# A graph network on one core: the second matmul of a tile takes a one-hot of its own

## The chip, the cores and the metric

The kernel runs on one core of one Trainium2 chip. The core has TensorE (PE, with its weight loads shown apart as PEld), VectorE (DVE), ScalarE (ACT), GpSimd (POOL) and SyncE (SP), and 16 DMA engines that move data between the chip's DRAM and the on-chip memories SBUF and PSUM. The metric is device time in microseconds (us). The kernel before takes 2262.35 us in the median of 3 runs (2259.93 to 2263.4).

## The reference

There are 6250 nodes with 128 features, and 200000 edges with 128 features, sorted by destination node. Cut to what matters:

```python
def l0(node, edge, src, dst, W, b):
    agg_src = segment_sum(node[src], dst, num_segments=6250)
    agg_edge = segment_sum(edge, dst, num_segments=6250)
    h = concatenate([node, agg_src, agg_edge], axis=1)
    return relu(h @ W.T + b)

def sage(x, src, dst, W_l, b_l, W_r):
    agg = segment_sum(x[src], dst, num_segments=6250)
    deg = segment_sum(ones(200000), dst, num_segments=6250)
    return (agg / maximum(deg, 1.0)[:, None]) @ W_l + b_l + x @ W_r

h = maximum(layernorm(x), 0)
x = x + l0(h, edge_attr, src, dst, W0, b0)
h = maximum(layernorm(x), 0)
h = relu(sage(h, src, dst, W1_l, b1, W1_r))
x = x + relu(sage(h, src, dst, W2_l, b2, W2_r))
```

All three layers sum over the same edges. The destinations are drawn as 6250 times the square of a uniform number, so low nodes have many edges and high nodes few.

## The kernel before

**Two halves.** The first half (to about 940 us) builds a matrix of counts in DRAM, `counts_d`: how many edges lead from each source to each destination. Sources are split as source = 128 x block + place, with NB = 49 blocks; partition is the place, and a column is destination x 49 + block. The second half reads these counts back, 128 destinations at a time (L578), and multiplies them with the node terms (L584), once per layer; the matrix product does the gathering and the summing.

**How counts are built.** Edges come in 196 groups of 8 tiles of 128 edges. Per group, VectorE makes two one-hot arrays (`onehots`, L389 to L396): `sp` has, for each edge, a one at the source's place (128 columns); `sq` has a one at (destination - first destination of its window) x 49 + block, `nq` = 49 x w columns. TensorE multiplies them (L504): sp transposed times sq is the table of counts for a window of w nodes. ScalarE casts it from PSUM (`pu`, three buffers) into a strip in SBUF, the ring (L531 or L536), at an offset that it loads into a register (`to_put`, L489, through L384). There are three rings of SWMAX = 148 nodes. After a *stretch* of some groups SyncE writes the ring to `counts_d` (L559), at a place in DRAM that comes from a register too; the next stretch takes the next ring. Writes overlap in their nodes, and the later must come later, so each waits until the one before has landed.

**Regions.** The list is cut into 14 regions of 14 groups. REGIONS (L36) gives for each: tiles to a window (n), nodes in a window (w), groups in a stretch (k), nodes in a ring written (sw), and the width of the window for edge sums. In regions 0 to 5 a window holds 4 or 2 tiles; GpSimd adds the first node of a window to what the ring has there already (L534), and at a seam between stretches it copies that node over from the old ring (L481). In regions 6 to 13 (from G1 = group 84 on) a window holds one tile (n == 1). There the first node of a window may have edges in the tile before as well, and a **second matmul** (L515 to L522) adds that tile's counts of this node on top in PSUM, over NB = 49 columns: it takes the `sp` of the tile before, and of its `sq` the 49 columns that start at an offset. The offset is (first node of this tile - first node of the tile before) x 49. It is known only from the data, so TensorE loads the eight offsets of a group into registers, one group ahead (L544 to L548, through L384, from the list `step_i` made at L302 to L307).

**Around it.** Edge features are summed with matmuls as well: `edge_sums` (L398) loads a tile of 1024 edges (SP, three buffers), makes a one-hot `hot` (DVE, L405), does eight f32 matmuls (L414) and adds to `aggE` (DVE, L419). It is fed in between the count matmuls by share of the work (L541, L542): a group of n == 1 counts twice. Every third group a block of 128 nodes goes through the layer norm and the first layer's products (`first_layer`, until group 145), on all engines. The order on each engine is not the program's text: a planner puts the instructions of the whole program in order by its own estimate of durations, and each engine then works in that order, with semaphores between engines. Pools open and close (`setup`, `build`), so a later tile may lie where an earlier one lay: the rings, whose first memset is L375, lie where tiles of the setup lay.

## Time and profile before

| | |
|---|---|
| median of 3 runs | 2262.35 us |
| the profiled execution's own time | 2267.7 us |
| its span, first to last instruction | 2266.0 us |
| busy: PE, PEld | 2067.5 us, 1693.1 us |
| busy: DVE, ACT, POOL | 1207.9 us, 791.9 us, 217.9 us |
| DMA moved | 478.93 MB, of it 447.53 MB through SyncE's queue |
| mean granted TensorE clock | 0.982 |
| last counts write issued | 934.2 us |
| first load of counts (L578) | 940.0 us |

The profile shows one execution. A row of its groups reads: line, engine, operation, what is written and read, shapes, number; then busy time and the mean duration of one in ns; then how long the engine stood idle just before these instructions and what ended most of that. "issue" as what ended it means that no semaphore was waited for. A letter q behind an engine (ACTq, SPq, PEldq) is that engine's sequencer: register loads, waits and DMA issues are done there and are not counted as busy. Times of PE are modelled at their ends, so a matmul of 490 columns, shown with 0.37 us, lets the next one start after 0.2 us.

### The profile page before, as it was taken

What the parts mean: (1) busy time and instruction counts of PE and PEld (TensorE: products, weight loads), DVE (VectorE), ACT (ScalarE), POOL (GpSimd) and SP (SyncE); (2) the same over time, 40 slices, a digit from 0 to 9 for tenths busy, and PEclk for the clock granted to TensorE, in tenths of its full rate; (3) what the DMA queues carried; (4) which work ended last, traced back from release to release, by engine and by line L of the source; (5) the groups of instructions that cost most, each with busy time, mean ns of one, the idle gap of its engine ahead of it and who ended that gap; (6) DMA issues with size and microseconds to landing.
All of it is one profiled execution on the core that took longest, in us unless ns stands there. A gap on an engine that the chain in (4) does not pass through costs nothing.

```text
span 2266.0 us, 39466 instructions
## 1 busy us (share of the span) xinstructions
PE 2067.5 (91%) x13713; PEld 1693.1 (75%) x13713; DVE 1207.9 (53%) x2296; ACT 791.9 (35%) x2010; POOL 217.9 (10%) x421
## 2 busy tenths in 40 slices
PE   6977778898888888779999999999999999999998
PEld 5865557777666666567888887778888888888887
DVE  8987765677666666475555555444444431111111
ACT  3565566788888787311111111111111110000000
POOL 5666650000000000100000000000000000000000
PEclk9999999999999999899999999999999999999999
DMA  3554566777777677745555555555555556666663
GB/s 116 187 170 166 187 222 227 254 273 263 250 254 266 243 257 258 271 157 205 209 204 202 200 199 196 180 192 186 191 204 191 185 200 218 228 227 229 226 226 135
DMA packets 140315, 478.93 MB, mean 211 GB/s; under 512 B 15249, under 2 KB 85967, under 8 KB 114384
## 3 DMA queue, kind: packets, MB, share of 16 engines
q1 hardware_dynamic: 81540, 447.53, 55.5%
q10 hardware_dynamic: 57996, 27.16, 4.2%
q8 instruction: 115, 1.88, 0.3%
q0 software_dynamic: 576, 1.63, 0.2%
q14 instruction: 88, 0.72, 0.1%
HBM read 362.19 MB, written 114.08 MB: 210 GB/s over the span
## 4 chain that ended last, share of the span: by engine, by line
PE 61%; issue 10%; DVE 10%; DMA 9%; ACT 6%; ACTq 2%; POOLq 1%; POOL 1%; DVEq 0%; SPq 0%
PE ps L584 37%; PE pe L414 12%; PE pu L504 7%; DMA c<-counts_d 6%; ACT ring L531 3%; PE pz L344 2%; DVE high L592 2%; DVE sq L391 1%; DVE worse L593 1%; PE pu L516 1%; ACTq L384 1%; DMA edge_t<-in_edge 1%; PE pt L341 1%; ACT ring L536 1%; ACT h L334 1%
## 5 line engine op out<-in xcount | busy, mean ns | idle before, releaser
L584 PE MATMUL ps<-terms,c 128*128 128x384 bf16 (+1 forms) x7203 | 1228.3, 327 | 13.1 <-DMA c<-counts_d 13.1
L584 PEld LDWEIGHTS <-c 128*128 128x128 bf16 x7203 | 1020.5, 142 | 180.6 <-issue 18.8
L414 PE MATMUL pe<-hot,edge_t 128*128 128x128 f32 x3136 | 517.9, 294 | 19.9 <-DMA edge_t<-in_edge 12.8
L531 ACT CAST ring<-pu 128x490 f32 (+6 forms) x891 | 470.3, 534 | 108.2 <-PE pu L516 69.9
L414 PEld LDWEIGHTS pe<-hot,edge_t 128*128 128x128 f32 x3136 | 419.0, 195 | 78.6 <-issue 32.3
L504 PE MATMUL pu<-sq,sp 128*128 128x512 bf16 (+7 forms) x1782 | 396.3, 315 | 34.1 <-ACT ring L536 16.1
L391 DVE TENSOR_TENSOR sq<-iota,q_e 128x3136 bf16<-128x3136 f16 (+8 forms) x196 | 353.2, 1802 | 0.0
L595 DVE TENSOR_REDUCE y<-ps 128x128 f32<-128x384 f32 x147 | 81.2, 553 | 384.7 <-PE ps L584 384.7
L504 PEld LDWEIGHTS <-sp 128*128 128x128 bf16 x1782 | 176.3, 100 | 140.5 <-issue 84.2
L391 DVE TENSOR_TENSOR sp<-iota,p_e 128x1024 bf16<-128x1024 f16 x196 | 136.2, 695 | 172.3 <-PE pu L516 154.8
L516 PE MATMUL pu<-sq,sp 128*128 x892 | 163.5, 186 | 64.4 <-issue 63.6
L534 POOL TENSOR_TENSOR ring<-ring,fore 128x49 f32 x280 | 173.5, 620 | 89.9 <-ACT fore L526 30.3
L593 DVE TENSOR_REDUCE worse<-high 128x1 f32<-128x3136 bf16 x49 | 167.5, 3419 | 1.6
L347 DVE TENSOR_TENSOR r<-pz,b_sb 128x128 f32<-128x128 f32 x98 | 28.6, 292 | 226.8 <-ACT terms L345 226.8
L536 ACT CAST ring<-pu 128x196 f32 (+5 forms) x280 | 112.0, 404 | 71.9 <-issue 34.9
L330 ACT ACTIVATE rstd<-mv,eps 128x1 f32<-128x1 f32 x98 | 29.0, 300 | 287.2 <-DVE mv L328 287.2
L516 PEld LDWEIGHTS <-sp 128*128 128x128 bf16 x892 | 87.4, 98 | 43.2 <-issue 12.6
L732 ACT ACTIVATE h<-y 128x128 f32<-128x128 f32 x49 | 15.1, 309 | 289.4 <-DVE y L724 289.4
L592 DVE TENSOR_TENSOR high<-c 128x3136 bf16<-128x3136 bf16 x49 | 87.7, 1790 | 49.4 <-DMA c<-counts_d 49.1
L405 DVE TENSOR_TENSOR hot<-iota,rel 128x64 f32<-128x64 f16 (+13 forms) x196 | 96.0, 492 | 0.6 <-POOL hot L375 0.6
L350 ACT CAST terms<-z 128x128 bf16<-128x128 f32 x147 | 44.0, 300 | 92.9 <-DVE z L349 92.1
L351 DVE TENSOR_TENSOR terms<-z,terms 128x128 bf16<-128x128 f32 x147 | 44.2, 301 | 59.6 <-ACT terms L350 59.3
(138 smaller groups left out, 820.7 us busy)
## 6 DMA issues: line engine op xcount, KB each, us to landing
c<-counts_d SPq DMA_DIRECT2D x147, 1568.0 KB, 6.4
edge_t<-in_edge SPq DMA_DIRECT2D x196, 512.0 KB, 3.7
counts_d<-ring SPq DMA_DIRECT2D x7, 1813.0 KB, 6.2
counts_d<-ring SPq DMA_DIRECT2D x7, 1715.0 KB, 6.5
counts_d<-ring SPq DMA_DIRECT2D x7, 1568.0 KB, 6.7
counts_d<-ring SPq DMA_DIRECT2D x7, 1445.5 KB, 5.7
own<-r_d ACTq DMA_DIRECT2D x147, 64.0 KB, 5.5
counts_d<-ring SPq DMA_DIRECT2D x7, 1298.5 KB, 6.2
```

Source lines behind the costliest of these rows:

```text
L391: nc.vector.tensor_tensor(to.rearrange("p t (c two) -> p t c two", two=2), iota[:, :m].rearrange("p (c two) -> p c two", two=2).unsqueeze( ...
L405: nc.vector.tensor_tensor(hot[:, :, :win], iota[:, :win].unsqueeze(1).to_broadcast([P, U, win]), rel[:, g, :].unsqueeze(2).to_broadcast([P ...
L414: mm = nc.tensor.matmul(ps[:, :P], e[:, u, :], hot[:, u, :], start=u == 0, stop=u == U - 1)
L504: mm = nc.tensor.matmul(pu[:, c:z], sp[:, t, :], sq[:, t, c - i * 512 : z - i * 512], start=t == t0, stop=t == t0 + n - 1 and (n > 1 or c ...
L516: mm = nc.tensor.matmul(pu[:, i * 512 : i * 512 + NB], sp_b[:, t, :], sq_b[:, t, bass.ds(step, NB)], start=False, stop=j0 == len(last_tile ...
L531: nc.scalar.copy(ring[:, bass.ds(to_put[t0], nq)], pu[:, i * 512 : i * 512 + nq])
L534: add = nc.gpsimd.tensor_tensor(to, to, fore[:, i, :], op=ALU.add)
L536: put = nc.scalar.copy(ring[:, bass.ds(to_put[t0 // n] + NB, nq - NB)], pu[:, i * 512 + NB : i * 512 + nq])
L584: nc.tensor.matmul(ps[:, :m], stands, moves, start=i == 0, stop=i == len(products) - 1)
L592: nc.vector.tensor_tensor(high, cf[:, :half], cf[:, half:], op=ALU.max)
L593: nc.vector.tensor_reduce(worse[:, 6 + b : 7 + b], high, AX.X, ALU.max)
L595: nc.vector.tensor_reduce(y, ps[:, : NK * D].rearrange("p (k f) -> p f k", k=NK), AX.X, ALU.add)
```

## The change

The diff does five things.

1. The second matmul takes its 49 columns not from the earlier tile's `sq` at an offset but from a new one-hot, `sc`, made by VectorE per group: 50 columns for each of 8 tiles (9 in the first group of n == 1). It compares the same `iota` with `carry`, which holds for each tile the index q of that tile less the step to the next tile's window. TensorE's register loads and the list `step_i` go.
2. `carry` is made once, by `carries()`, at group 14: two matmuls spread the steps from one partition over all 128, and three DVE operations subtract them from `q_e`.
3. The stretches of regions 1, 2, 3 are 7, 4, 3 groups (before: 14, 7, 7), and those of regions 8 to 13 one group (before: two). That makes 124 stretches where there were 76, each with its own write.
4. The rings hold 86 nodes where they held 148, and the nodes written per stretch (sw) shrink with them.
5. The steps are cut off at w and not at w - 1, since a step past the window now simply matches no column.

```diff
 REGIONS = (
     (4, 4, 14, 40, 8),
-    (4, 6, 14, 110, 12),
-    (2, 5, 7, 100, 18),
-    (2, 7, 7, 134, 22),
+    (4, 6, 7, 70, 12),
+    (2, 5, 4, 62, 18),
+    (2, 7, 3, 66, 22),
     (2, 8, 2, 60, 28),
     (2, 9, 2, 70, 32),
     (1, 6, 2, 74, 36),
     (1, 7, 2, 86, 42),
-    (1, 8, 2, 98, 46),
-    (1, 9, 2, 106, 52),
-    (1, 10, 2, 118, 56),
-    (1, 10, 2, 128, 62),
-    (1, 11, 2, 140, 68),
-    (1, 12, 2, 148, 74),
+    (1, 8, 1, 54, 46),
+    (1, 9, 1, 60, 52),
+    (1, 10, 1, 68, 56),
+    (1, 10, 1, 72, 62),
+    (1, 11, 1, 76, 68),
+    (1, 12, 1, 82, 74),
 )
-SWMAX = 148
+SWMAX = 86
...
-    step_i = lists.tile([1, (G - G1) * U], I32, name="step_i")
+    T1 = G1 * U
+    carry = lists.tile([P, GU - T1 + 1, 2], F16, name="carry")
+    steps = lists.tile([1, GU - T1], F32, name="steps")
...
-    steps = room.rearrange("o g u -> o (g u)")[:, : (G - G1) * U]
-    nc.vector.tensor_tensor(steps, flat(unit)[:, G1 * U :], flat(unit)[:, G1 * U - 1 : GU - 1], op=ALU.subtract)
+    nc.vector.tensor_tensor(steps, flat(unit)[:, T1:], flat(unit)[:, T1 - 1 : GU - 1], op=ALU.subtract)
     nc.vector.tensor_scalar(
-        steps, steps, float(max(r[3] for r in regions) - 1), float(NB), op0=ALU.min, op1=ALU.mult
+        steps, steps, float(max(r[3] for r in regions)), float(NB), op0=ALU.min, op1=ALU.mult
     )
-    nc.vector.tensor_scalar(step_i, steps, 0.0, None, op0=ALU.max)
...
+    def carries():
+        ones = small.tile([1, P], F32, name="ones", bufs=1)
+        nc.vector.memset(ones, 1.0)
+        flat_q = q_e.rearrange("p g u two -> p (g u) two")
+        pu = bpsum.tile([P, 2 * 512], F32, name="pu", bufs=3)
+        half = (GU - T1) // 2
+        assert half <= 512 and 2 * half == GU - T1
+        for i in range(2):
+            nc.tensor.matmul(
+                pu[:, i * 512 : i * 512 + half], ones, steps[:, i * half : (i + 1) * half], start=True, stop=True
+            )
+            nc.vector.tensor_tensor(
+                carry[:, 1 + i * half : 1 + (i + 1) * half],
+                flat_q[:, T1 - 1 + i * half : T1 - 1 + (i + 1) * half],
+                pu[:, i * 512 : i * 512 + half].unsqueeze(2).to_broadcast([P, half, 2]),
+                op=ALU.subtract,
+            )
+        nc.vector.tensor_tensor(
+            carry[:, 0:1], flat_q[:, T1 - 2 : T1 - 1], pu[:, 0:1].unsqueeze(2).to_broadcast([P, 1, 2]), op=ALU.subtract
+        )
...
         for g in range(g0, g0 + ng):
+            if g == RUN:
+                carries()
             sp = hots.tile([P, U, P], BF16, name="sp")
...
             else:
-                steps = steps_of.pop(g)
+                of_first = 2 if g == G1 else 1
+                sc = hots.tile([P, U + 1, NB + NB % 2], BF16, name="sc")
+                c0 = g * U - T1 + 1
+                onehots(
+                    sc[:, 2 - of_first : U + 1], carry[:, c0 + 1 - of_first : c0 + U], U + of_first - 1, NB + NB % 2
+                )
...
-                        step = steps[t0 if t0 != live[0] else 0]
-                        for j0, (sp_b, sq_b, t) in enumerate(last_tiles):
+                        slot = t0 + 1 if t0 != live[0] else 1
+                        for j0, (sp_b, t) in enumerate(last_tiles):
                             mm = nc.tensor.matmul(
                                 pu[:, i * 512 : i * 512 + NB],
                                 sp_b[:, t, :],
-                                sq_b[:, t, bass.ds(step, NB)],
+                                sc[:, slot + 1 - len(last_tiles) + j0, :NB],
                                 start=False,
                                 stop=j0 == len(last_tiles) - 1,
                             )
-                    last_tiles = [(sp, sq, t) for t in range(t0, t0 + n)]
+                    last_tiles = [(sp, t) for t in range(t0, t0 + n)]
...
-                if j == 0 and G1 <= g + 1 < G:
-                    steps_of[g + 1] = group_values(
-                        step_i[0:1, (g + 1 - G1) * U : (g + 2 - G1) * U], ET.PE, (max(r[3] for r in regions) - 1) * NB
-                    )
```

More of the change, by code (lines that the diff above doesn't have):

```diff
@@ L469 @@
     writes = []
-    steps_of = {}
     block = 0
```

## The prediction

> **What bounds the kernel now.** I read the page first (groups of instructions, then the forty slices), then the busy time of each engine by region of the edge list, then the waits inside the one-tile regions, then a timeline of a few microseconds there, and last the DMA issues.
>
> The span is 2266.0 us. From about 940 us on, TensorE works through L584 at 0.9 to 1.0 busy; nothing of the change is in there. The change acts before 940 us, where the counts are built, and most of it in the last eight of the fourteen regions (313 to 936 us), where a window holds one tile (n == 1).
>
> ```profile
> L504 PEld LDWEIGHTS <-sp 128*128 128x128 bf16 x1782 | 176.3, 100 | 140.5 <-issue 84.2
> L516 PE MATMUL pu<-sq,sp 128*128 x892 | 163.5, 186 | 64.4 <-issue 63.6
> L531 ACT CAST ring<-pu 128x490 f32 (+6 forms) x891 | 470.3, 534 | 108.2 <-PE pu L516 69.9
> ```
>
> TensorE stood idle for 64.4 us just before L516, the second matmul, and for no semaphore ("issue"). ScalarE, which copies the windows out, waited 69.9 us for that same matmul. The stages, one line per region (the columns are PE, weight load, DVE, ACT, POOL, granted clock, DMA share, GB/s; here regions 6 to 13):
>
> ```profile
> 313.00:387.50 74.50, 61.28 (x514) 50.76 (x515) 41.74 (x106) 48.97 (x141) 7.11 (x19) 1.00 0.71 245
> 387.50:457.00 69.50, 61.93 (x523) 52.43 (x520) 44.03 (x95) 54.00 (x137) 0.00 (x0) 0.98 0.74 253
> 457.00:525.00 68.00, 61.72 (x524) 51.50 (x522) 47.62 (x93) 58.26 (x134) 0.00 (x0) 1.00 0.79 272
> 525.00:599.70 74.70, 66.38 (x525) 52.98 (x524) 51.26 (x85) 62.94 (x133) 0.20 (x1) 0.98 0.72 251
> 599.70:678.20 78.50, 68.61 (x520) 51.85 (x517) 53.30 (x74) 63.97 (x122) 0.00 (x0) 0.98 0.72 254
> 678.20:757.20 79.00, 67.32 (x511) 50.75 (x510) 52.20 (x64) 63.12 (x113) 0.00 (x0) 0.98 0.73 256
> 757.20:842.20 85.00, 73.55 (x614) 57.59 (x613) 55.30 (x62) 67.24 (x112) 0.00 (x0) 0.98 0.71 256
> 842.20:936.00 93.80, 79.31 (x648) 61.87 (x647) 59.97 (x65) 73.94 (x115) 3.12 (x1) 0.98 0.67 245
> ```
>
> TensorE is nearest to full, ScalarE stands close behind it, VectorE has 20 to 34 us to spare in each region. What the idle time is shows in the timeline of TensorE around 710 us and in the register loads there:
>
> ```profile
> 709.05 0.37 PE L504 MATMUL pu<-sq,sp 128*128 128x490 bf16 x1
> 710.59 0.18 PE L516 MATMUL pu<-sq,sp 128*128 x1 [1.17 <-issue]
> ```
> ```profile
> L384 PEldq TENSOR_LOAD <-step_i x1: 1881/1881/1881, 708.5 to 708.5; - x1
> L384 ACTq TENSOR_LOAD <-at_i x1: 1523/1523/1523, 710.3 to 710.3; - x1
> ```
>
> One load of eight registers per group stood 1.88 us in TensorE's queue and the second matmul came 1.17 us late. ScalarE has such a load too (L384, its ring offsets), and that one stays. One group earlier the same two loads took 0.593 and 0.549 us. The difference is the counts write that SyncE issued at 706.82 us: loads that fall into such a write take 1.1 to 2.4 us, others 0.55 to 0.59; from 600 us on it is about every second one, as a stretch of two groups writes once.
>
> **The change, part by part.**
>
> 1. *TensorE's register loads go.* Waits of L516 for "issue", region by region: 3.6, 4.9, 6.0, 7.1, 8.8, 10.9, 11.1, 12.1 = 64.5 us, which is the page's row. A rule of the Trainium skill (Runtime: NRT & Kernel Launch, section Instruction fetch mechanics) prices such a load at about 200 ns a register, so 112 groups x 8 x 0.2 = 179 us of queue time; the trace has a median of 0.77 us per load, 112 x 0.77 = 86 us, and lets only 64 us of it through as idle matmul time. I take the trace; with the rule the gain would look nearly three times as large as TensorE can lose.
>
> 2. *ScalarE stands next.* Its floor per region is busy time, plus about 0.03 us between casts (seven of 0.57 us take 4.17 us), some 3 us a region, plus the gap of a fast load (0.19 us x 14 = 2.7 us): busy + 6. That gives 64.3, 68.9, 70.0, 69.1, 73.2, 79.9 us for regions 8 to 13, so 3.7 + 5.8 + 8.5 + 9.9 + 11.8 + 13.9 = 53.6 us to win; in regions 6 and 7 TensorE's own stall is the smaller, 3.6 + 4.9. Together 62 us if all of ScalarE's loads were fast. They will not be: with a write per group each load finds one nearby. Today it starts about 3.5 us after the issue of a write (706.82 to 710.3). The new writes hold 661 to 1004 KB and should be nearly out by then, so I take a mean of 0.75 us, 0.2 us over the fast one: 84 groups x 0.2 = 17 us, leaving 45. TensorE and ScalarE are then within 5% of each other with three PSUM buffers between them; I take off a fifth for their getting in each other's way. **Gain 36 us.** Bounds: 62 with all loads fast; 24 if every second one is still slow (28 x 1.15 = 32 us off 62, less a fifth).
>
> 3. *VectorE makes the second one-hot.* 8 x 50 = 400 elements a group. By the rows of the same operation, 1024 elements in 695 ns and 1568 in 1001 ns, 0.56 ns an element, 400 cost 0.34 us; x 112 = 39 us. It hides in VectorE's spare time (its "sp" waits 144.6 us for L516 in these regions). Without that cover it is the whole 39 us. Behind it in VectorE's queue stand the edge sums (L419, L405); TensorE waited about 2 us for L419 from 388 us on, so there is room. The second matmul itself, 128x49, costs what it cost, and the 892 register additions (42 to 46 ns on its sequencer) go unseen.
>
> 4. *carries(), once, at group 14:* two DVE subtractions of 896 elements (L303, 896 elements: 1.07 us) and a small one, 2.3 us; two f32 matmuls of 448 columns (L344, 256 columns: 0.41 us, so 0.72 each), 1.4 us. In that region PE (34.0) and DVE (34.1) are both busy for all of 35.0 us, so nothing hides it: **+2.5** (1.4 to 3.7).
>
> 5. *Shorter stretches in regions 1 to 3:* 2, 4 and 5 stretches where there were 1, 2 and 2, six more. Each brings a seam copy and a register load on POOL, a load and a write on SP, and behind that write the edge loads in SP's queue. Nearest rows: regions 2 and 3, two stretches each, took 43.0 and 48.0 us with windows of 5 and 7 nodes, 2.5 us a node; regions 4 and 5 (8 and 9 nodes, seven stretches each) would take 50.5 and 53 by that, and took 61 and 56. So 13.5 us for ten more stretches, 1.4 each: **+8.3** (3 to 20; at 202 us one such write held SP for 11 us, waiting for POOL).
>
> 6. *Shorter stretches in regions 8 to 13:* 84 writes for 42, 742 more nodes at 12.25 KB, 9 MB. A group of region 11 then moves 72 x 12.25 = 882 KB of counts and 1.27 edge tiles of 512 KB (20.4 records of L414 a group, 16 a tile) in some 5.1 us: about 310 GB/s where it is 256 now; the trace has moved 272 at a DMA share of 0.79. Each write waits in SP's queue for the group's last cast and for the write before it to land (L559 waited for counts_d 17.6 us, 12 times), and the edge loads wait behind. Three rings give a write two groups, about 10 us. What a write takes:
>
> ```profile
> counts_d<-ring SPq DMA_DIRECT2D x7, 1813.0 KB, 6.2
> ...
> counts_d<-ring SPq DMA_DIRECT2D x7, 1053.5 KB, 6.2
> ...
> counts_d<-ring SPq DMA_DIRECT2D x7, 857.5 KB, 4.2
> counts_d<-ring SPq DMA_DIRECT2D x7, 735.0 KB, 3.9
> ```
>
> Here the skill speaks against the change: DMA: Bandwidth & Descriptors, section Bandwidth, asks for transfers of 1 MiB and more, and its formula (section Anatomy of one DMA, SWDGE) is about 2 us plus bytes over 436 GB/s. That makes 6.3 us of one write of 1813 KB and 2 x 4.4 us of two of 1004.5. By the formula a write still lands inside its group (3.6 to 4.4 us against 4.6 to 5.7), so the sum stays at nothing. The row at 1053.5 KB, 6.2 us amid edge loads, is less kind: at that landing the writes would set the pace. I take 4 to 5.5 us, between the rows, and **0**.
>
> 7. *Ends.* VectorE loses step_i (L307, 0.6 us) just ahead of the first one-hot. The first ring's memset (L375, 3.13 us of POOL) falls to 86/148 of that, and the padded tiles behind it, for which TensorE waits 1.8 us at L414, come 1.3 us sooner: **-1.9**. The last write, 1004.5 for 1813 KB, lands about (1813 - 1004.5) x 2.1 us per 1000 KB = 1.7 us sooner, and the first load of L578 waits for it: **-1.7**.
>
> Sum: -36 + 2.5 + 8.3 - 1.9 - 1.7 = -28.8 us. The profiled execution took 2267.7 us (span 2266.0) and would take 2238.9; on the median of 2262.35, **2234 us**.
>
> **The rivals.**
>
> *A: ScalarE keeps its slow loads* (0.14). For it: every group now has a write. Against: the writes are half as long. Gain 24 instead of 36: 2246 us.
>
> *B: the chain of writes sets the pace, slower than before* (0.18). One write per group, each waiting for the one before to land. Regions 8 to 13 now take 479 us for 84 groups, 5.7 us each; with the small terms about cancelling (regions 6 and 7 gain 8.5, parts 4, 5 and 7 cost 7.2), a landing above 5.7 us decides it. At 6.2 us: 84 x 6.2 = 521, +42 us, near 2303; at 5.9, 2278. For it: the row at 1053.5 KB. Against: all six of these writes are smaller, and 857.5 KB took 4.2.
>
> *C: VectorE's one-hot is late* (0.08): TensorE waits for sc instead of for registers. If the 39 us come uncovered, 36 - 39 leaves +10 us, 2272; if half, 2253.
>
> *D: all loads fast, seams cheap* (0.08): 62 x 0.9 - 3 - 2.5 + 3.6 = 54, 2208 us.
>
> *That it does not do what it says* (in C): no register of TensorE is left in the diff, so its loads must vanish; only the time may not.
>
> **How the numbers follow.** The forecast has 0.52, with its own range 2218 to 2250. Over 0.2% (4.5 us), about what a measurement can tell from no change, is above 2267 or below 2258. Faster: the forecast, D, most of A, a little of C: 0.72. Slower: B mostly, half of C: 0.20. Same: 0.08. Leaving out one in ten at each side, the range goes down to 2210 (half of D's side) and up to 2276 (the nearer part of B).
>
> **What would show it.** Part 1: no L384 on TensorE, no "issue" wait at L516. Part 2: regions 10 to 13 shorter by 6 to 12 us each, ScalarE with under 8 us idle in each, PE waiting for ACT at L504. Part 3: a row of 128x400 at 0.34 us. Part 5: regions 1 to 3 longer by some 8 us, POOL seam copies 25 instead of 19. Part 6: landings of 4 to 5.5 us; B would show as SP waiting for counts_d before each L559 and PE waiting for edge_t. Wrong also if the order of instructions, planned anew for the whole program, moves a stall into the stages after 940 us, which I take as unchanged at 1326 us.

## The result and the profile after

The changed kernel takes 2237.36 us (median of 4 runs, 2235.33 to 2239.14); the kernel before took 2262.88 us beside it. The ratio is 0.9905, with a 95% interval of 0.9886 to 0.9925: 1% faster, as forecast (2234 us). A second group of runs gives 0.9916 (0.9897 to 0.9935). The profiled execution has a span of 2235.4 us, 30.6 us less than before's 2266.0.

The total was close; its parts were not all so. First the groups of instructions of the changed kernel (L534 is the first matmul of a window, L546 the second, L561 ScalarE's cast; the columns as in the page before):

```profile
L561 ACT CAST ring<-pu 128x490 f32 (+6 forms) x891 | 469.5, 534 | 96.9 <-PE pu L546 43.0
L534 PE MATMUL pu<-sq,sp 128*128 128x512 bf16 (+7 forms) x1782 | 387.0, 313 | 55.9 <-ACT ring L561 26.7
L546 PE MATMUL pu<-sc,sp 128*128 128x49 bf16 x892 | 163.1, 186 | 0.0
```

The second matmul waits for nothing (0.0 us) where it waited 64.4 us. Part of TensorE's wait has moved to the first matmul, which now waits for ScalarE. In the kernel before its row (L504) was

```profile
L504 PE MATMUL pu<-sq,sp 128*128 128x512 bf16 (+7 forms) x1782 | 396.3, 315 | 34.1 <-ACT ring L536 16.1
```

The stages of the changed kernel, one line for each of regions 6 to 13, then the stretch from the last cast to the first late matmul (the first of L609, which reads counts), then the rest, called the late half below (columns: PE, weight load, DVE, ACT, POOL, granted clock, DMA share, GB/s):

```profile
317.40:390.80 73.40, 61.53 (x528) 53.41 (x527) 48.82 (x129) 48.36 (x142) 4.14 (x10) 0.98 0.72 245
390.80:468.10 77.30, 66.33 (x524) 54.86 (x523) 48.87 (x110) 51.09 (x134) 0.00 (x0) 0.93 0.65 225
468.10:538.30 70.20, 64.36 (x533) 52.81 (x532) 52.96 (x112) 58.58 (x137) 0.20 (x1) 1.00 0.80 278
538.30:609.20 70.90, 66.56 (x514) 50.59 (x513) 54.68 (x95) 62.28 (x133) 0.00 (x0) 1.00 0.81 282
609.20:683.40 74.20, 70.06 (x529) 51.61 (x528) 57.51 (x90) 64.44 (x120) 0.00 (x0) 1.00 0.82 289
683.40:755.10 71.70, 66.67 (x502) 48.44 (x500) 56.13 (x78) 63.63 (x113) 0.00 (x0) 1.00 0.85 306
755.10:835.00 79.90, 75.55 (x627) 57.99 (x626) 59.66 (x77) 68.28 (x113) 0.00 (x0) 0.98 0.78 285
835.00:913.00 78.00, 72.37 (x588) 54.36 (x585) 56.19 (x72) 68.73 (x107) 1.77 (x1) 1.00 0.78 285
913.00:928.30 15.30, 0.00 (x0) 0.01 (x1) 0.00 (x0) 0.02 (x1) 1.89 (x4) 0.59 0.71 278
928.30:2235.40 1307.10, 1280.22 (x7596) 1065.12 (x7596) 541.93 (x1123) 134.93 (x441) 5.86 (x52) 0.99 0.57 203
```

A region is read from ScalarE's first cast in it to that of the next region; before's lines in the prediction were cut by eye, so its regions are cut again the same way for the table. "Again" is a second profiled execution of the same kernel. In the forecast's column the gain of 36 us is spread in proportion over the region gains of 62 that it was taken from.

| stage, us | before | before again | after | after again | after minus before | forecast |
|---|---|---|---|---|---|---|
| start to first cast | 42.1 | 42.2 | 39.4 | 39.5 | -2.7 | -1.9 |
| regions 0 to 5 | 278.1 | 277.9 | 278.0 | 280.7 | -0.1 | +10.8 |
| regions 6 and 7 | 141.4 | 140.9 | 150.7 | 150.6 | +9.3 | -4.9 |
| region 8 | 68.7 | 68.5 | 70.2 | 69.9 | +1.5 | -2.1 |
| regions 9 to 13 | 403.8 | 399.3 | 374.7 | 371.3 | -29.1 | -29.0 |
| last cast to first late matmul | 13.1 | 12.4 | 15.3 | 15.3 | +2.2 | -1.7 |
| the late half | 1318.8 | 1312.0 | 1307.1 | 1305.2 | -11.7 | 0 |
| span | 2266.0 | 2253.2 | 2235.4 | 2232.5 | -30.6 | -28.8 |

So regions 9 to 13 did as forecast, regions 6 to 8 went the other way, and regions 0 to 5, which were to lose 11 us, and the late half, which was to stay as it was, made that up. The experiments ask which of these belong to which part of the change, and which to one execution alone.

### The profile page after: what moved, and what is told of

Same layout as the page of the kernel before. It is cut to its first block, busy times and chain, and to the rows that moved or that the text cites. A ratio compares the mean times of both kernels' runs of the same rounds, so it can differ in the third digit from the quotient of the medians.

```text
span 2235.4 us, 38803 instructions
## 1 busy us (share of the span) xinstructions
PE 2073.7 (93%) x13717; PEld 1691.1 (76%) x13717; DVE 1242.0 (56%) x2419; ACT 789.2 (35%) x2011; POOL 205.0 (9%) x427
## 4 chain that ended last, share of the span: by engine, by line
PE 60%; ACT 13%; DMA 9%; DVE 8%; issue 6%; ACTq 2%; POOLq 0%; SPq 0%; POOL 0%; DVEq 0%
PE ps L609 44%; ACT ring L561 10%; PE pe L437 6%; PE pu L534 5%; DMA counts_d<-ring 4%; DMA c<-counts_d 3%; PE pz L344 2%; ACTq L384 1%; DMA edge_t<-in_edge 1%; DVE sq L391 1%; DVE worse L618 1%; PE pt L341 1%; DVE high L617 1%; ACT h L334 1%; DVE sp L391 1%
## 5 line engine op out<-in xcount | busy, mean ns | idle before, releaser
L609 PE MATMUL ps<-terms,c 128*128 128x384 bf16 (+1 forms) x7203 | 1226.7, 327 | 16.9 <-DMA c<-counts_d 16.9
L609 PEld LDWEIGHTS <-c 128*128 128x128 bf16 x7203 | 1019.9, 142 | 183.6 <-issue 21.7
L437 PE MATMUL pe<-hot,edge_t 128*128 128x128 f32 x3136 | 521.0, 294 | 33.5 <-DMA edge_t<-in_edge 17.1
L561 ACT CAST ring<-pu 128x490 f32 (+6 forms) x891 | 469.5, 534 | 96.9 <-PE pu L546 43.0
L437 PEld LDWEIGHTS pe<-hot,edge_t 128*128 128x128 f32 x3136 | 418.2, 195 | 70.2 <-issue 18.1
L534 PE MATMUL pu<-sq,sp 128*128 128x512 bf16 (+7 forms) x1782 | 387.0, 313 | 55.9 <-ACT ring L561 26.7
L534 PEld LDWEIGHTS <-sp 128*128 128x128 bf16 x1782 | 175.6, 100 | 99.4 <-issue 33.6
L564 POOL TENSOR_TENSOR ring<-ring,fore 128x49 f32 x280 | 161.8, 578 | 102.3 <-ACT fore L556 36.1
L546 PE MATMUL pu<-sc,sp 128*128 128x49 bf16 x892 | 163.1, 186 | 0.0
L391 DVE TENSOR_TENSOR sp<-iota,p_e 128x1024 bf16<-128x1024 f16 x196 | 135.4, 691 | 21.8 <-PE pu L534 16.9
L546 PEld LDWEIGHTS <-sp 128*128 128x128 bf16 x892 | 87.0, 98 | 70.2 <-issue 38.5
L566 ACT CAST ring<-pu 128x196 f32 (+5 forms) x280 | 112.3, 403 | 67.9 <-issue 39.5
L617 DVE TENSOR_TENSOR high<-c 128x3136 bf16<-128x3136 bf16 x49 | 87.6, 1789 | 42.1 <-DMA c<-counts_d 42.1
```

Of the source, the lines that this page charges most:

```text
L391: nc.vector.tensor_tensor(to.rearrange("p t (c two) -> p t c two", two=2), iota[:, :m].rearrange("p (c two) -> p c two", two=2).unsqueeze( ...
L437: mm = nc.tensor.matmul(ps[:, :P], e[:, u, :], hot[:, u, :], start=u == 0, stop=u == U - 1)
L534: mm = nc.tensor.matmul(pu[:, c:z], sp[:, t, :], sq[:, t, c - i * 512 : z - i * 512], start=t == t0, stop=t == t0 + n - 1 and (n > 1 or c ...
L546: mm = nc.tensor.matmul(pu[:, i * 512 : i * 512 + NB], sp_b[:, t, :], sc[:, slot + 1 - len(last_tiles) + j0, :NB], start=False, stop=j0 == ...
L561: nc.scalar.copy(ring[:, bass.ds(to_put[t0], nq)], pu[:, i * 512 : i * 512 + nq])
L564: add = nc.gpsimd.tensor_tensor(to, to, fore[:, i, :], op=ALU.add)
```

## The experiments

Each group of runs has its own runs of the kernel before on the same chip; the ratio is always to those. Ratios are compared across groups, medians only within one.

### One part alone: the new one-hot with the long stretches

The diff is against the changed kernel. The rings hold 140 nodes, not the 148 of the kernel before, and region 13 keeps its one group to a stretch and its 82 nodes.

```diff
-    (1, 8, 1, 54, 46),
-    (1, 9, 1, 60, 52),
-    (1, 10, 1, 68, 56),
-    (1, 10, 1, 72, 62),
-    (1, 11, 1, 76, 68),
+    (1, 8, 2, 98, 46),
+    (1, 9, 2, 106, 52),
+    (1, 10, 2, 118, 56),
+    (1, 10, 2, 128, 62),
+    (1, 11, 2, 140, 68),
...
-SWMAX = 86
+SWMAX = 140
```

with regions 1 to 3 as before, too.

> The second one-hot as changed, the stretches as before except in region 13 (one group each, 82 nodes) and rings of 140 nodes. Theory (the register loads are what is won, ScalarE stands next): most of the gain without the cost of short stretches, but every second ScalarE load slow as before: 2235 to 2245 us. If short stretches are what helps (by making ScalarE's loads fast): under 10 us of gain, 2253 or more. If short stretches only cost: 2220 to 2232.

Measured: 2244.64 us, ratio 0.9955 (0.9937 to 0.9972).

### The other part alone: the short stretches with TensorE's register loads

```diff
-    (1, 8, 2, 98, 46),
+    (1, 8, 1, 54, 46),
...
-SWMAX = 148
+SWMAX = 86
```

This is the kernel before with the whole REGIONS table of the changed one.

> The kernel before with the changed REGIONS and rings of 86 nodes; TensorE keeps its register loads and its offset into sq. Theory: with TensorE's stall in place the faster loads still shorten that stall in regions 8 to 13 (about 0.3 us a group, 25 us), six more seams cost some 8, and the stage after the counts gains what it gained in the changed kernel if that comes from the width of counts_d: 2235 to 2262 us. If the gain is all the one-hot's: 2265 or more.

Measured: 2242.76 us, ratio 0.9946 (0.9931 to 0.9961).

### TensorE's loads away, nothing put in their place

```diff
-                        step = steps[t0 if t0 != live[0] else 0]
...
-                                sq_b[:, t, bass.ds(step, NB)],
+                                sq_b[:, t, NB : 2 * NB],
```

The second matmul takes 49 fixed columns, so the sums of first nodes are not the reference's; no one-hot is added.

> The kernel before, but the second matmul reads sq at one fixed offset (the second node's columns), so that TensorE loads no register; the sums of a window's first node are therefore not the reference's. No second one-hot, stretches as before. Theory: what the loads alone cost TensorE is 64 us of idle time, of which ScalarE lets 25 to 40 through: 2222 to 2238 us. If the one-hot on VectorE costs much in the changed kernel, this one is faster than that by 10 us or more.

Measured: 2247.55 us, ratio 0.9964 (0.9952 to 0.9977): a miss, some 10 us above the expected range.

What follows from the three. Regions 10 to 13 took 327.3 us before (323.8 in the second execution). The waits of TensorE in these regions (total us, times, longest), first in the kernel before, then in the three kernels above in their order, last in the changed kernel:

```profile
PE pu L516 <- issue: 41.9, 36, 2.8
PE pu L504 <- ACT ring L531: 2.2, 7, 0.6
```
```profile
PE pu L534 <- ACT ring L561: 31.6, 44, 1.5
```
```profile
PE pu L516 <- issue: 24.4, 37, 1.6
PE pu L504 <- ACT ring L531: 6.9, 12, 1.5
```
```profile
PE pu L502 <- ACT ring L528: 36.4, 48, 1.7
```
```profile
PE pu L534 <- ACT ring L561: 15.9, 29, 2.3
```

Without TensorE's loads (the first and third of the three) most of the 41.9 us comes back as a wait for ScalarE, and the regions fall only to 312.9 and 318.8 us. With the stretches shortened and the loads kept (the second) the "issue" wait itself falls to 24.4 us and the regions take 312.5. Both together give 303.8. In the whole time the two gains add: 0.45% and 0.54%, and 0.84 to 0.95% together.

By region it is less even, as the first kernel has the short stretches in region 13. In regions 10 to 12 (239.6 us in the second execution of before) each part alone takes 4.5 us off, and both together 13.8 (15.7 in the second execution of the changed kernel, 8.8 in the kernel further down with long stretches in regions 1 to 3): at least the sum. In region 13 (84.2 us) the short stretches do it alone: 77.4 us with TensorE's loads kept, 77.8 and 78.0 without them.

What shortening alone changes is the length of the register loads in this stretch of time. First the kernel before, then short stretches alone (duration in ns: least, median, longest):

```profile
L384 PEldq TENSOR_LOAD <-step_i x55: 587/1048/2950, 609.4 to 928.9; - x55
L384 ACTq TENSOR_LOAD <-at_i x55: 536/550/2315, 611.0 to 929.6; - x55
```
```profile
L384 PEldq TENSOR_LOAD <-step_i x55: 587/593/1872, 605.0 to 910.3; - x55
L384 ACTq TENSOR_LOAD <-at_i x55: 541/549/2208, 606.8 to 910.9; - x55
```

The mean of these loads, worked out over the 55, falls from 1.30 to 0.89 us on TensorE and from 1.14 to 0.80 us on ScalarE; in the changed kernel ScalarE's is 0.66 (0.71 in its second execution). Which loads are long goes by the last counts write. In the kernel before, the 28 loads of TensorE that start 1.6 to 4.3 us after such a write was issued take 1.05 to 2.95 us; of the other 27, which start later, 26 take 0.59 to 0.60. With the shorter writes those that start from 3.3 us on take 0.59 to 0.68 us. So the shorter stretches, which the forecast counted for ScalarE's loads and otherwise only at a price, are worth about as much alone as the removal of TensorE's loads.

### Only the width of the table in DRAM

```diff
-    counts_d = dram.tile([P, (NP + SWMAX) * NB], BF16, name="counts_d")
+    counts_d = dram.tile([P, (NP + 148) * NB], BF16, name="counts_d")
```

The changed kernel with the rows of `counts_d` as wide as before; every engine's order of instructions is that of the changed kernel.

> The changed kernel, only the DRAM matrix counts_d as wide as before (6420 instead of 6358 nodes in a row); every engine's instructions and their order are the same. The stage after the counts took 1318.8 us before and 1307.1 after, with nothing changed in it. If the row's width is the cause: that stage goes back towards 1318, 2245 to 2250 us in all. If it is the order of instructions: no difference, 2235 to 2240 us.

Measured: 2243.39 us, ratio 0.995 (0.9934 to 0.9965); the late half takes 1308.5 us in its profiled execution (span 2237.0), the changed kernel's 1307.1. The width is not where the late half's difference comes from. The ratio is 0.34 points above that of the next run, which was made on another chip; whether the chip or the width makes that, these runs don't tell.

### The changed kernel once more

> The changed kernel itself once more, beside the other three of this set: a second profile, to tell what moves from one execution to the next. Expected 2235 to 2243 us; the stage after the counts 1307 to 1309 us; regions 4 and 5 within 6 us of 109; region 7 again about 77 us, if its loss belongs to the order of instructions.

Measured: 2236.88 us, ratio 0.9916 (0.9897 to 0.9935). Its stages are in the table above. Regions 6 to 8 repeat to 0.4 us, and the waits that lengthen them (below) stand at the same places: what happens there belongs to the kernel, not to one execution.

### The kernel before once more

> The kernel before once more, for its stages. In the profile of before the half after the first late matmul took 1318.8 us; in seven other kernels, whose late half is the same text, it took 1302.7 to 1308.7 us. If that was this one execution's own (theory 1), it takes 1302 to 1310 us here, regions 4 and 5 together take 110 to 117 us, regions 6 and 7 138 to 145, regions 8 and 9 140 to 147, regions 10 to 13 322 to 330, and the span is 2248 to 2258 us. If it belongs to before's order of instructions (theory 2), it takes 1316 to 1321 us again.

Measured: 2254.89 us in this run, span 2253.2. Its stages are in the table above; the two that differ most from the first profile, regions 9 to 13 and the late half:

```profile
529.50:928.80 399.30, 345.38 (x2769) 267.02 (x2767) 266.85 (x339) 326.58 (x582) 3.12 (x1) 0.99 0.72 256
...
941.20:2253.20 1312.00, 1282.31 (x7596) 1064.83 (x7596) 542.37 (x1123) 135.16 (x441) 5.85 (x52) 0.99 0.57 202
```

Regions 0 to 8 repeat to 0.9 us; the late half takes 6.8 us less than in the first profile and regions 9 to 13 take 4.5 us less.

The 4.5 us go with TensorE's clock. Regions 9 and 10, in the first profile and then in the second (the granted clock is the third number from the end):

```profile
530.30:606.80 76.50, 67.57 (x531) 53.41 (x529) 51.60 (x81) 63.30 (x133) 0.00 (x0) 0.98 0.73 253
606.80:684.40 77.60, 68.28 (x519) 51.65 (x519) 53.22 (x74) 63.69 (x120) 0.00 (x0) 0.98 0.72 253
```
```profile
529.50:605.00 75.50, 66.20 (x531) 52.17 (x530) 51.51 (x82) 63.29 (x132) 0.00 (x0) 1.00 0.73 257
605.00:680.90 75.90, 66.62 (x519) 50.62 (x519) 53.05 (x74) 63.73 (x119) 0.00 (x0) 1.00 0.73 259
```

The first execution has one stretch of 3.4 us at half clock in each of regions 9 to 13, the second only in 11 and 12. Regions 9, 10 and 13 are 1.0, 1.7 and 1.8 us longer in the first; regions 11 and 12 differ by 0.1 us at most. Each of these stretches follows a wait of L516 for its registers of 1.3 to 2.8 us.

The late half has 22 us at half clock in both executions, so its 6.8 us are something else. Neither theory fits it: 1312.0 lies between. More than half of its 11.7 us was the first execution's own, or its chip's, and some 5 us, against the 1307.1 of the changed kernel, stay open. Most of it is one kind of wait, that of the matmul at L341 for ScalarE's h: 29.0 and 22.8 us in the two executions of before, 19.9 and 19.7 in those of the changed kernel. Why it differs is not shown. In the twelve other profiles the late half takes from 1302.7 to 1308.7 us with the same text in it.

### VectorE's new work taken away

```diff
-                sc = hots.tile([P, U + 1, NB + NB % 2], BF16, name="sc")
+                if g == G1:
+                    sc = hots.tile([P, U + 1, NB + NB % 2], BF16, name="sc", bufs=1)
+                    onehots(sc, carry[:, : U + 1], U + 1, NB + NB % 2)
...
-                onehots(
-                    sc[:, 2 - of_first : U + 1], carry[:, c0 + 1 - of_first : c0 + U], U + of_first - 1, NB + NB % 2
-                )
```

> The changed kernel with the second one-hot made once, in the first group of one-tile windows, and used by all groups; the sums of first nodes are therefore not the reference's. It takes 39 us of VectorE's work away. Theory 1 (part 3 of the forecast: that work is hidden): within 4 us of the changed kernel, 2233 to 2241 us, regions 6 and 7 at 147 to 153 us as before. Theory 2 (VectorE's extra work makes edge sums and sq late in regions 6 and 7, where TensorE waited 7.0 us for aggE and 3.5 us for VectorE's one-hots): regions 6 and 7 fall to 140 to 144 us and the whole to 2226 to 2231 us. If VectorE's one-hot were late everywhere (rival C), the whole would fall by 15 us and more, below 2222 us.

Measured: 2238.24 us, ratio 0.9908 (0.9877 to 0.994), the changed kernel's. Regions 6 and 7 do fall, to 145.9 us, about as theory 2 has it, but regions 0 to 5 take 287.2 us, and regions 0 to 8 together 501.1 us (501.2 in the second execution of the changed kernel). In the whole time no cost of VectorE's one-hot can be told, and rival C, which would show as 15 us and more, falls.

### Regions 1 to 3 with their long stretches

```diff
-    (4, 6, 7, 70, 12),
-    (2, 5, 4, 62, 18),
-    (2, 7, 3, 66, 22),
+    (4, 6, 14, 110, 12),
+    (2, 5, 7, 100, 18),
+    (2, 7, 7, 134, 22),
...
-SWMAX = 86
+SWMAX = 134
```

> The changed kernel with the stretches of regions 1 to 3 as they were before (14, 7 and 7 groups, rings of 134 nodes). Forecast (part 5: six more stretches cost 8.3 us): regions 1 to 3 go from 131 to about 123 us and the whole to about 2228 us. Rival, from the lengths of these regions in the runs so far (128.2 to 130.6 us with long stretches, 129.9 to 132.2 us with short ones): the six stretches cost 1 to 2 us, and the whole stays at 2233 to 2238 us; larger rings put the first memset back (POOL 1.5 us more), which takes 1 us of it back.

Measured: 2241.82 us, ratio 0.9916 (0.9884 to 0.9947). Regions 1 to 3 take 130.5 us; the changed kernel's two executions 132.2 and 130.4. Six more stretches cost less than 2 us, not 8.3, and taking them away gains nothing in the whole time.

### A fourth buffer for the edge tiles

```diff
-    edges = build.enter_context(tc.tile_pool(name="edges", bufs=3))
+    edges = build.enter_context(tc.tile_pool(name="edges", bufs=4))
```

> The changed kernel with four buffers for edge tiles in place of three. TensorE waits 17.1 us for edge tiles in the changed kernel, and 4.4 us in regions 6 and 7. If late edge tiles are what regions 6 and 7 lose: those waits nearly vanish, 10 to 15 us less than the changed kernel. If they only stand in for VectorE's and ScalarE's lateness: the wait moves to another name and the time stays within 4 us.

Measured: 2228.3 us, ratio 0.9869 (0.985 to 0.9887): 8.6 us below the changed kernel on the same chip. What it takes away stands among TensorE's waits before region 8 of the changed kernel (its second execution):

```profile
PE pe L437 <- DMA edge_t<-in_edge: 19.4, 8, 4.7
PE pu L534 <- ACT ring L566: 15.5, 18, 1.9
PE pe L437 <- DVE aggE L442: 7.7, 11, 1.5
PE pe L437 <- DVE st L326: 7.3, 2, 3.9
```

With four buffers no wait for edge_t is left among the seven longest kinds there; part of it comes back as waits for ScalarE (23.2 us at the same cast, L566). Regions 0 to 7 take 423.3 us instead of 431.3. Regions 8 to 13, though, take 447.3 instead of 441.2.

### ScalarE's register loads away in the one-tile regions

```diff
-            to_put = group_values(places, ET.Activation, (sw - w) * NB)
+            if n > 1:
+                to_put = group_values(places, ET.Activation, (sw - w) * NB)
...
-                        nc.scalar.copy(ring[:, bass.ds(to_put[t0], nq)], pu[:, i * 512 : i * 512 + nq])
+                        nc.scalar.copy(ring[:, t0 * NB : t0 * NB + nq], pu[:, i * 512 : i * 512 + nq])
```

The casts go to fixed places, so the counts of these regions are not the reference's.

> The changed kernel, but in the regions with one tile to a window ScalarE writes each window at a fixed place of the ring and loads no register, so the counts are not the reference's. If ScalarE is the bound there after the change and its loads are the rest of it: regions 8 to 13 lose most of the 0.2 us a group that the shortest load leaves as a gap and 0.1 more, 84 x 0.3 = 25 us, 2210 to 2220. If TensorE or the transfers bound them: under 8 us.

Measured: 2192.77 us, ratio 0.9712 (0.9693 to 0.9731), 44 us below the changed kernel and 17 below the expected range. Regions 10 to 13 take 291.3 us where it has 301.6, and regions 6 and 7 (first line; the second is what ScalarE waits for from region 8 on):

```profile
334.10:449.00 114.90, 114.71 (x1039) 103.07 (x1039) 95.35 (x223) 102.46 (x272) 0.41 (x1) 1.00 0.83 292
```
```profile
ACT ring L562 <- DMA counts_d<-ring: 18.7, 19, 3.0
```

TensorE has no idle time left in regions 6 and 7. Regions 0 to 5 take 294.7 us here, 14 more than with the loads, so the net of regions 0 to 7 is -22 us. Much of the 14 is the clock: regions 0 to 5 hold 40.8 us at half clock here and 19.0 in the changed kernel (second execution), which by half of the difference, an estimate, is up to 11 us. The planner makes a different order for this kernel, and how much of the 22 us is the loads and how much the order is not settled. From region 8 on the next thing in the way shows: ScalarE waits for a ring whose write has not landed.

### The last cast of a group on VectorE

```diff
+                        if k == 1 and t0 == U - 1:
+                            v = value(at_i[0:1, g * U + t0 : g * U + t0 + 1], ET.DVE, (sw - w) * NB)
+                            nc.vector.tensor_copy(ring[:, bass.ds(v, nq)], pu[:, i * 512 : i * 512 + nq])
+                            continue
```

The changed kernel with one of eight casts, from region 8 on, moved from ScalarE to VectorE.

> The changed kernel, with one of the eight casts of a group in regions 8 to 13 done by VectorE (its last tile), which has about 1 us to spare in a group. If ScalarE is the bound: 0.3 us a group less, about 25 us, 2212 to 2222. If VectorE's waits for ScalarE in its own queue make its one-hots late: no gain, or up to 15 us slower than the changed kernel.

Measured: 2217.72 us, ratio 0.9825 (0.9807 to 0.9843): 19.2 us below the changed kernel on the same chip. The moved casts on VectorE (durations in ns, then the shapes), what ScalarE then waits for in regions 8 to 13 (total us, times, longest), and that stage:

```profile
L563 DVE CAST ring<-pu x84: 557/666/775, 473.6 to 896.3; 128x490 f32 x28, 128x392 f32 x14, 128x441 f32 x14, 128x539 f32 x14
```
```profile
ACT ring L565 <- DMA counts_d<-ring: 35.9, 32, 3.9
```
```profile
469.90:895.00 425.10, 404.58 (x3279) 314.53 (x3278) 382.48 (x599) 341.53 (x635) 1.98 (x2) 0.99 0.84 301
```

Regions 8 to 13 go from 441.2 to 425.1 us up to ScalarE's last cast; VectorE's last one ends at 897.1, which makes it 427.2. ScalarE did stand next after TensorE's loads, as the prediction's part 2 had it, and 84 casts off it give 14 to 16 us there. Behind it stand the writes: 35.9 us of waiting for a ring, where the changed kernel (second execution, same regions) has 9.7 us.

### Both: the split casts and four edge buffers

> The changed kernel with both: VectorE casts the last tile of each group in regions 8 to 13 (it gained 19 us alone) and four edge buffers (8.6 us alone, in regions 0 to 7 and the late half). Theory 1 (different regions, so the gains add): 2237 - 19 - 8 = 2206 to 2214 us. Theory 2 (in regions 8 to 13 the counts writes now set the pace, ScalarE having waited 36 us for a free ring, and earlier edge loads stand in their way): only the larger gain is left, 2215 to 2220 us.

Measured: 2219.15 us, ratio 0.9819 (0.9795 to 0.9843); the edit is the two above together. The gain of the fourth buffer is gone. Regions 6 and 7, then 8 to 13:

```profile
321.40:460.80 139.40, 121.52 (x1049) 103.48 (x1048) 97.06 (x238) 99.26 (x276) 3.71 (x11) 1.00 0.74 254
460.80:894.80 434.00, 405.43 (x3279) 314.80 (x3277) 382.82 (x599) 341.86 (x635) 1.98 (x2) 0.99 0.83 294
```

Regions 6 and 7 take 10.1 us less than with three buffers (149.5), with no stretch at half clock where there were 13.7 us of it, and regions 8 to 13 take 8.9 us more (425.1). The outcome is theory 2's. The place where it is given back is shown, and it is the same with the fourth buffer alone (6.1 us more there); that earlier edge loads delay the writes is only argued, ScalarE's wait for a ring having grown by just 2.3 us, to 38.2. Both kernels with split casts beat the changed kernel and the one before; between them no difference can be told.

## Why the prediction was right, and where it was not

The total came out 3 us from the forecast, and that is in part luck: errors of opposite sign cancelled. The main term, a gain of 36 us in regions 6 to 13, came out at 18.3 us (613.9 us before, 595.6 after; 16.9 between the second executions). Regions 6 to 8 came out 18 us above their forecast (10.8 for -7.0) and the two ends together 3 us; regions 0 to 5 came out 8 to 11 us below theirs, and the late half, which was to stay, 5 us (12 in the first profile). The medians fell by 25.5 and 20.0 us in the two groups of runs. Rival D had its two premises nearly right, loads mostly fast and seams cheap, and was still 29 us off, as it too saw nothing but ScalarE behind TensorE's stall.

**Part 1, TensorE's loads: right.** No load is left on TensorE in the one-tile regions, and L546 waits 0.0 us. Two readings of its working were off without bearing on the result: 112 loads at the median of 0.77 us make 86 us, but their sum in the profile is 128.1 us, and the long ones reach 2.95 us, not 2.4.

**Part 2, ScalarE stands next: right in its sum from region 9 on, wrong in regions 6 to 8.** Regions 9 to 13 fell by 29.1 us, 29.0 in the forecast (24.6 to 28.0 against the second execution of before). The forecast's term for ScalarE's loads was a mean of 0.75 us; from 609 us on they have

```profile
L384 ACTq TENSOR_LOAD <-at_i x55: 542/548/1752, 613.5 to 909.0; - x55
```

with a mean of 0.66, so rival A (every second one still long) falls. The reason given, that shorter writes are nearly out when the load starts, is half of it: 24 of these 55 loads start 3.3 us or more after the issue of the last write, but 24 others start within 0.6 us of the issue of a write, before or after, and are short as well. Only the seven between take 0.79 to 1.75 us.

The two terms behind the 29 us were both a little off, in opposite ways. The loads cost 0.11 us over the short ones, 70 groups x 0.11 = 7.7 us in these regions, where 0.2 made 14. Of the 49.9 - 7.7 = 42.2 us then left, 29.1 came. But the prediction's cut by eye takes in 5.3 us of region 8 and 1.9 us after the last cast; by the table's cuts 47.2 us were there to win (42.7 by the second execution of before), and the two engines' getting in each other's way took 0.20 to 0.30 of what was left, where the forecast had a fifth. It shows in regions 10 to 13 as 15.9 us of TensorE's waiting for ScalarE. The signs named for these regions did not all come: they fell by 3.4, 7.2, 4.9 and 8.0 us, not by 6 to 12 each, and ScalarE is idle for 8.1 to 11.6 us in each, not under 8.

A part of the 29.1 us is one that the prediction did not have. Regions 9 to 13 hold 17.1 us at half clock before (6.8 in the second execution) and 3.4 after (0 in the second). By half of the difference, an estimate, that is up to 7 us (3 between the second executions): half clock came behind TensorE's waits for registers, and went with them.

In regions 6 to 8 the step that failed is "in regions 6 and 7 TensorE's own stall is the smaller, 3.6 + 4.9", as if nothing else stood close behind that stall. The 7.5 us of "issue" did go. Others came; the waits of regions 6 and 7 in the changed kernel:

```profile
PE pe L437 <- DVE aggE L442: 7.0, 9, 1.5
...
PE pe L437 <- DMA edge_t<-in_edge: 4.4, 2, 3.2
...
PE pu L534 <- ACT ring L561: 3.9, 8, 1.1
...
PE pe L437 <- DVE st L326: 3.5, 1, 3.5
```

Before, the wait for aggE was 3.3 us; those for an edge tile and for ScalarE were 0.9 and 1.6 us, and the one that VectorE's statistics (st) end was not there. And the long ones among them cost more than their own length. One of them, in TensorE's timeline, and the same moment in stages:

```profile
397.69 0.77 PE L437 MATMUL pe<-hot,edge_t 128*128 128x128 f32 x2 [3.23 <-DMA edge_t<-in_edge]
```
```profile
390.80:397.00 6.20, 3.66 (x34) 3.09 (x32) 4.19 (x12) 4.64 (x11) 0.00 (x0) 1.00 0.90 320
397.00:403.80 6.80, 6.11 (x28) 4.95 (x28) 0.48 (x1) 1.33 (x3) 0.00 (x0) 0.50 0.03 11
```

After a wait of 3.2 us TensorE's granted clock is 0.50 for 6.8 us. The Trainium skill (TensorE: Matmul & The Clock Gate, section Part 1: The HAM clock gate) says that the clock falls to half after about 3.4 us of idling; by that this gap of 3.2 us would have cost no more than itself. Here gaps shorter than that were followed by half clock as well. In the four profiles of the kernels before and after, between the first cast and the last, TensorE's gaps of 1.5 to 2 us were followed by a stretch at half clock within 4 us in 4 cases of 39, those of 2 to 3 us in 11 of 19, and those above 3 us in 14 of 15. In regions 6 to 8 the changed kernel spends 13.7 us at half clock in both its executions, the kernel before 3.4 and 6.0 us. By half of the difference, an estimate, that is 4 to 5 us of the time, and TensorE's busy time in regions 6 and 7 grew by as much (123.3 to 127.9 us). With 4.7 us more idle time it makes the 9.3 us.

Why the waits moved there is not shown. The prediction named a new order of instructions as what could make it wrong, but only for the late half. The lengthening belongs to the kernel, since regions 6 to 8 take 220.9 and 220.5 us in its two executions and 217.6 in the one with wide rows, where the order is the same. But neither part alone brings it: with TensorE's loads gone and nothing added they take 209.1 us, with the one-hot and long stretches 210.6, with the loads kept and short stretches 211.3, where the kernel before takes 210.1 and 209.5. With VectorE's one-hot taken away from the changed kernel they take 213.9, with a fourth edge buffer 216.4. Each of these five kernels has an order of its own, so these runs can't tell the order from the work in it.

**Part 3, the second one-hot: right.** 361 ns in the median (0.34 forecast), and no cost of it in the whole time.

**Part 4, carries(): of the right size.** In the two kernels that have carries() and the long stretches in regions 1 to 3, regions 0 and 1 take 70.4 and 67.9 us against 67.2 before: 3.2 and 0.7 us more (2.5 forecast). Of the 3.2 all but 0.6 us is made good by the end of region 5.

**Part 5, shorter stretches in regions 1 to 3: wrong.** Less than 2 us instead of 8.3. The step that failed is "regions 4 and 5 would take 50.5 and 53 by that, and took 61 and 56. So 13.5 us for ten more stretches": the difference was put down to seams alone. TensorE's waits in before name others: in regions 4 and 5 it waits 14.6 us for ScalarE's casts and 8.8 us for edge tiles, in regions 2 and 3 8.4 and 3.2. That is 11.8 us more, nearly all of the 13.5. A line through two regions was no measurement of a seam.

**Part 6, the writes: right as the time goes, but nearer than thought.** The DMA issues:

```profile
counts_d<-ring SPq DMA_DIRECT2D x21, 735.0 KB, 3.8
counts_d<-ring SPq DMA_DIRECT2D x14, 1004.5 KB, 5.4
counts_d<-ring SPq DMA_DIRECT2D x14, 931.0 KB, 4.7
counts_d<-ring SPq DMA_DIRECT2D x14, 882.0 KB, 4.6
counts_d<-ring SPq DMA_DIRECT2D x14, 833.0 KB, 4.9
...
counts_d<-ring SPq DMA_DIRECT2D x14, 661.5 KB, 3.7
```

Landings of 3.7 to 5.4 us were forecast as 4 to 5.5 (the prediction's estimate by the formula of the Trainium skill, DMA: Bandwidth & Descriptors, section Anatomy of one DMA, about 2 us plus bytes over 436 GB/s, was 3.6 to 4.4, up to 1 us short), against 5.3 us for a group (444.9 us for 84); so rival B fell, by a small margin. Of the 742 nodes more that the working counts for regions 8 to 13, 140 belong to regions 1 to 3. SyncE now waits much more for the write before:

```profile
SPq L584 <- DMA counts_d<-ring: 70.6, 50, 3.9
```

That is 70.6 us in 50 waits from region 7 on, where the whole of regions 6 to 13 had 2.8 us in 3 before (the prediction's 17.6 us in 12 waits are those of the whole kernel), and it is what the split casts run into.

**Part 7, the ends: half right.** The start fell by 2.7 us (1.9 forecast). The smaller rings alone bring the first cast from 42.1 to 42.0 us, and the one-hot with larger rings to 42.3, so the split into its two terms is not shown. The end was to gain 1.7 and lost 2.2 us. Its step took the last write to start with the last cast, as before (934.2 us against 934.1). Now the chain of writes is behind: the last cast ends at 913.0 us, the last write leaves at 917.6, and the first load of counts at 921.5.

**The late half: assumed unchanged, and about so.** The base of the sum, one execution with a late half of 1318.8 us, was some 7 us high there; the median it was set against was not.

## What to carry to other kernels

When a queue's register load is long, look at what is in flight when it runs: here making the transfers shorter won as much as removing the loads. Before spending a stall's idle time in full, list the other waits of that engine in the same stretch of time and redo the sum with each of them on the path. Look at the granted clock before comparing two stages or two executions: of TensorE's waits of 2 us and more, 25 of 34 had a stretch at half clock behind them here. And take a cost per piece from an experiment or from a piece's own rows, not from the difference of two stages that differ in other ways as well.

## What the runs showed of the hardware

A register load of eight values takes 0.55 us on ScalarE and 0.59 us on TensorE, and in the kernel before, from region 10 on, up to 2.95 us when it starts 1.6 to 4.3 us after the issue of a write of 1.4 to 1.8 MB from SBUF. The loads of both engines are hit alike, and halving the writes took the excess of TensorE's mean over 0.59 us from 0.71 to 0.30 us. Gaps of TensorE of 2 to 3 us were followed by half clock in 11 of 19 cases, and such a stretch of 3.4 us made a region 1.0 to 1.8 us longer. One profiled execution of a kernel differed from another by 6.8 us in a stage of 1300 us, with the same time at half clock, and by 4.5 us in one of 400, with 10 us more of it, while other stages agreed to within 1 us.
